# Cross-attention on one core: one load queue in order of use, 40 idle transposes, and the last context rows turned between A and U

## The chip, the cores and the metric

The kernel runs on one core of one Trainium2 chip. The metric is device time in microseconds (us) of that core for one execution. Three runs of the kernel before gave 289.30, 289.48 and 289.98 us, a median of 289.48 us.

## What is computed

A cross-attention layer with a residual and a layer norm, in float32, over 16 batches, with 256 queries and 77 context rows for each and 8 heads of width 256. The mask of the inputs is all ones.

```python
Q = (x @ Wq).reshape(B, -1, H, D)            # x: (16, 256, 256), Wq: (256, 2048)
K = (ctx @ Wk).reshape(B, -1, H, D)          # ctx: (16, 77, 192), Wk: (192, 2048)
V = (ctx @ Wv).reshape(B, -1, H, D)          # Wv: (192, 2048)
score = einsum('bhqd,bhkd->bhqk', Q, K) / sqrt(256)    # heads moved ahead of the rows
attn = softmax(where(mask, score, -inf))
out = einsum('bhqk,bhkd->bqhd', attn, V).reshape(B, -1, H * D) @ Wo + x
y = (out - mean(out)) * rsqrt(var(out) + 1e-5) * gamma + beta
```

## The kernel before

The products of the weights are formed first, so that the big activations meet small matrices only. For each head, G = Wk Wq^T / 16 (192 x 256) stands for the query and key projections, and U = Wv Wo (192 x 256) for the value and output projections. Then, for four batches at a time, "A" is the context times G (77 columns for each head and batch); the scores of a batch are x times A, and the output is the probabilities times (context times U).

The work is in two stages. The first, the prologue, loads all weights, forms G and U, turns the context so that its columns lie on the partitions, and prepares A for the first four batches. The second, the loop over batches at L639, does scores, softmax, attention and layer norm; the prologue ends at about 61 us of 288.

The order of all engines is written by hand (`manual_schedule`, L80): each engine runs its instructions in the order of the program, and a tile framework adds the semaphore waits. Loads go through DMA instructions issued by the SP queue (SyncE) or, for one weight block, by the ACT queue. The framework counts their landings on eight semaphores taken in turn, so the ninth DMA can't be issued until the first has landed: at most eight loads are in flight.

The prologue, with the lines that matter here:

- `ident` is built on POOL; 28 transposes of `ident` into a bank that nobody reads follow on PE (L477-478).
- The weights Wk and Wq come in four column blocks a = 0..3 of four pieces each (`wk_nat`, 96 KB a piece, and `wq_nat`, 128 KB a piece; `load_qk`, L442-445). Block 0 of Wk is issued by ACT at the same time as block 0 of Wq by SP; all else is on SP.
- The context `c_sb` comes in two parts: its first three row blocks of 112 rows (252 KB, `load_c(0, first)`, L456) serve the first four batches; the other eight (672 KB, L459) the rest. Then come Wv (`wvT`, 16 pieces of 96 KB, L467), Wo (`wo_all`, 4 of 512 KB, L469), the mask (`bias`, 616 KB as broadcast), and x for the first group (`xT`).
- `wo_all` lies in the same memory as `wq_nat` (tag "w128"), so its first load waits until DVE has turned the last block of Wq.
- `turn_qk(a)` (L488) transposes block a of both weights in 32 x 32 blocks on DVE. `turn_v` (L514) does so with Wv.
- `turn_c(lo, hi)` (L495) turns row blocks of the context: transposes on PE into `pc` (L501), a copy to `cA` on ACT, one to the upper half of `cB` on DVE, and a copy of that to the lower half on POOL (L512).
- The loop over j = 0, 1 (L565) forms G for two of the four blocks (`pg`, L524, and `ph`, L538), scales it out of PSUM (`gA` on ACT, `gB` on DVE), and prepares half of A of the first four batches (`pa`, L184 and L198, then copies that alternate between ACT and DVE). For j = 0 the first context rows are turned between the two halves of `pg`, and at the end the remaining rows are turned (L593), followed on POOL by `cRA`, `cRB` (the last 13 keys of each batch) and a memset of `vr`.
- U follows (`pu`, L524, and `pw`, L538), and copies of `uB` on ACT, DVE and POOL (L619). POOL also makes `bias` from the mask (L602), ahead of the `uB` copies.
- `prepare_last` (L251) multiplies `cRA`/`cRB` with U into `pr` and copies it into `vr`.

PSUM is one ring of eight banks (`ps_mm`), taken in order.

```python
        load_qk(0, (nc.scalar, nc.sync))
        load_qk(1, (nc.sync, nc.sync))
        load_c(0, first)
        load_qk(2, (nc.sync, nc.sync))
        load_qk(3, (nc.sync, nc.sync))
        load_c(first, NCR)
```

Of the kernel before, what the change touches and what calls it, by code (L numbers as in the profile page):

```python
# [20 lines left out]
KM = 64  # L21
# [23 lines left out]
def kernel(  # L45
# [13 lines left out]
    nc = tc.nc  # L59
# [4 lines left out]
    NCR = B * S2 // CR  # L64
# [4 lines left out]
    NF = H // 2  # L69
    KR = S2 - KM  # L70
    BK = 32
    NM = P // BK
# [30 lines left out]
    cA = const.tile([P, B, S2], F32, tag="cA", name="cA")  # L103
    cB = const.tile([P, B, S2], F32, tag="cB", name="cB")
    cRA = const.tile([P, B, KR], F32, tag="cRA", name="cRA")
    cRB = const.tile([P, B, KR], F32, tag="cRB", name="cRB")
    vr = const.tile([P, B, DI], F32, tag="vr", name="vr")
# [13 lines left out]
    def flat(ap):  # L121
        return ap.rearrange("p a b -> p (a b)")
# [4 lines left out]
    def load_x(g):  # L127
        xg_of[g] = const.tile([P, GT, DI], F32, tag=f"xg{g}", name=f"xg_{g}")
        nc.sync.dma_start(xg_of[g], x_rows[:, g * GT : (g + 1) * GT, :])
# [3 lines left out]
    def evacuate(dst, src):  # L133
        evacs[0] += 1
        if evacs[0] % 2:
            nc.scalar.copy(dst, src)
        else:
            nc.vector.tensor_copy(dst, src)
# [295 lines left out]
    with tc.tile_pool(name="wonce", bufs=1) as wp:  # L434
        c_sb = wp.tile([CR, NCR, DL], F32, tag="c", name="c_sb")

        wq_nat = wp.tile([P, NF, DI // BK, P], F32, tag="w128", name="wq_nat")
        wk_nat = wp.tile([P, NF, NL, P], F32, tag="w96", name="wk_nat")
        wq_blocks = wq.rearrange("(m r) (a i f) -> a i r m f", r=BK, a=NF, i=NM)
        wk_blocks = wk.rearrange("(m r) (a i f) -> a i r m f", r=BK, a=NF, i=NM)  # L440

        def load_qk(a, queues):  # L442
            for queue, nat, blocks in zip(queues, (wk_nat, wq_nat), (wk_blocks, wq_blocks)):
                for i in range(NM):
                    queue.dma_start(nat[i * BK : (i + 1) * BK, a], blocks[a, i])

        def load_c(lo, hi):
            nc.sync.dma_start(c_sb[:, lo:hi, :], c_rows[:, lo:hi, :])

        first = -(-GB * S2 // CR)  # L450
        load_qk(0, (nc.scalar, nc.sync))

        warm = wp.tile([P, 1], F32, tag="warm", name="warm")
        nc.scalar.activation(warm, eps, AF.Exp)
        load_qk(1, (nc.sync, nc.sync))
        load_c(0, first)  # L456
        load_qk(2, (nc.sync, nc.sync))
        load_qk(3, (nc.sync, nc.sync))
        load_c(first, NCR)  # L459

        wvT = wp.tile([P, NF, NL, P], F32, tag="wvT", name="wvT")
        wo_all = wp.tile([P, NF, 4, DI], F32, tag="w128", name="wo_all")
        wv_blocks = wv.rearrange("(m r) (a i f) -> a i r m f", r=BK, a=NF, i=NM)
        wo_rows = wo.rearrange("(a p n) f -> a p n f", p=P, n=4)
        for a in range(NF):
            for i in range(NM):
                nc.sync.dma_start(wvT[i * BK : (i + 1) * BK, a], wv_blocks[a, i])  # L467
        for a in range(NF):
            nc.sync.dma_start(wo_all[:, a], wo_rows[a])  # L469
        nc.sync.dma_start(  # L470
            bias_f.bitcast(I32), mask.rearrange("b k -> (b k)").partition_broadcast(P)
        )
# [1 line left out]


        idle = ps_mm.tile([P, P], F32, tag="mm", name="idle")
        for i in range(28):  # L477
            nc.tensor.transpose(idle, ident, ident)


# [7 lines left out]
        def turn_qk(a):  # L488
            for nat, of in ((wk_nat, wkT_of), (wq_nat, wqT_of)):
                nc.vector.transpose(  # L490
                    of[a // 2][:, a % 2].rearrange("p n (m r) -> p m n r", r=BK),
                    nat[:, a].rearrange("p m (n c) -> p m n c", c=BK),
                )

        def turn_c(lo, hi):  # L495
            for r in range(lo, hi, 2):
                n = min(2, hi - r)
                pc = ps_mm.tile([P, 4, P], F32, tag="mm", name=f"pc_{r}")
                for lc in range(2):
                    for j in range(n):  # L500
                        nc.tensor.transpose(  # L501
                            pc[:, 2 * lc + j, :CR],
                            c_sb[:, r + j, lc * LB : lc * LB + P],
                            ident[:CR, :CR],
                        )
                rows = slice(r * CR, (r + n) * CR)
                evacuate(flat(cA)[:, rows].rearrange("p (j m) -> p j m", m=CR), pc[:, :n, :CR])
                evacuate(
                    flat(cB)[LB:, rows].rearrange("p (j m) -> p j m", m=CR),
                    pc[LB:, 2 : 2 + n, :CR],  # L510
                )
                nc.gpsimd.tensor_copy(flat(cB)[:LB, rows], flat(cB)[LB:, rows])  # L512

        def turn_v(a):  # L514
            blocks = wvT[:, a].rearrange("p m (c n) -> p m n c", n=4)
            nc.vector.transpose(blocks, blocks)
# [3 lines left out]
        def of_pair(out, a, weight, moving):  # L520

            for n in range(4):
                for e in range(2):
                    nc.tensor.matmul(  # L524
                        out[e][:, a % 2, :],
                        weight(a, e, n)[:, :P],
                        moving(a, e, n),
                        start=(n == 0),
                        stop=(n == 3),
                    )  # L530

        def rest_of_pairs(j, weight, moving, name):

            banks = [ps_mm.tile([P, DI], F32, tag="mm", name=f"{name}_{j}_{e}") for e in range(2)]
            for n in range(4):
                for i in range(2):
                    for e in range(2):
                        nc.tensor.matmul(  # L538
                            banks[e][half(i)],
                            weight(2 * j + i, e, n)[:, P:],  # L540
                            moving(2 * j + i, e, n),
                            start=(n == 0),
                            stop=(n == 3),
                        )
            return banks

        def two_banks(name, j):
            return [ps_mm.tile([P, 2, DI], F32, tag="mm", name=f"{name}_{j}_{e}") for e in range(2)]
# [16 lines left out]
        for j in range(NF // 2):  # L565
            pg = two_banks("pg", j)
            of_pair(pg, 2 * j, wk_part, wq_part)
            if j == 0:
                turn_c(0, first)
            of_pair(pg, 2 * j + 1, wk_part, wq_part)  # L570
            for e in range(2):
                nc.scalar.mul(gA_of[:, j, e], pg[e], D ** -0.5)
            for e, ph in enumerate(rest_of_pairs(j, wk_part, wq_part, "ph")):
                nc.vector.tensor_scalar(gB[:, 2 * j + e, :], ph, D ** -0.5, None, ALU.mult)
            if j == 0:
                turn_qk(2)
            else:
                turn_v(0)
                turn_v(1)
                for g in range(NG):  # L580
                    load_x(g)
                    if g == 0:
                        nc.sync.dma_start(gam, gamma.partition_broadcast(P))
                        nc.sync.dma_start(bet, beta.partition_broadcast(P))
            part_A, part_B, copies = prepare_a(0, (2 * j, 2 * j + 1))
            part_A()
            part_B()
            for i, (dst, src) in enumerate(copies()):
                evacuate(dst, src)
                if j == 0 and i == 3:  # L590
                    turn_qk(3)
            if j == 0:
                turn_c(first, NCR)  # L593
                nc.gpsimd.tensor_copy(cRA, cA[:, :, KM:])
                nc.gpsimd.tensor_copy(cRB, cB[:, :, KM:])
                nc.gpsimd.memset(vr, 0.0)
        turn_v(2)
        turn_v(3)

# [13 lines left out]
        for j in range(NF // 2):  # L613
            for e, pw in enumerate(rest_of_pairs(j, wv_part, wo_part, "pw")):
                for i, engine in enumerate((nc.scalar.copy, nc.vector.tensor_copy)):
                    a = 2 * j + i
# [118 lines left out]
```

## Time and profile before

| | |
|---|---|
| median of three runs | 289.48 us |
| the profiled execution: its time | 289.93 us |
| its span, first to last instruction | 288.1 us |
| PE busy | 275.2 us (96%) |
| DVE, ACT, POOL busy | 216.9, 113.1, 119.1 us |
| mean granted TensorE clock | 0.985 |
| loads and stores | 22.51 MB |

A line of a timeline gives the start and the length in us, the engine, the line of the kernel, the operation, what it writes and reads, the shapes and the number of instructions; the bracket at its end gives the idle time before it and what ended that. A line of the chain of waits gives start, length and what the end of the execution depended on in that stretch. A line of a table of windows gives, for a stretch of the span, each engine's busy time (and number of instructions), the granted TensorE clock (1.00 is full), the mean busy share of the 16 DMA engines and the rate of all transfers in GB/s. PE is matrix multiplication, PEld the loading of its weights, SPq and ACTq the queues that issue DMAs.

### The profile page before, as it was taken

To read this page: it belongs to the slowest core of one execution; us is meant where nothing else is said; L and a number is where in the kernel's file an instruction comes from. 1 tells how busy PE (TensorE), PEld (TensorE's weight loads), DVE (VectorE), ACT (ScalarE), POOL (GpSimd) and SP (SyncE) were. 2 spreads that over 40 slices of the span, in tenths; PEclk is the share of its full clock that TensorE was granted. 3 is DMA by queue.
4 is the path that set the end of the run, shared out by engine and by line. 5 is a ranking of instruction groups with operands and counts; after the bars stand their busy time and mean duration, and the time that the engine had idled before them with its cause. 6 is when DMAs were issued, how large, how long until landed. Compare 5 with 4: busy or idle time off the path is not lost.

```text
span 288.1 us, 11561 instructions
## 1 busy us (share of the span) xinstructions
PE 275.2 (96%) x5234; PEld 180.5 (63%) x5234; DVE 216.9 (75%) x421; ACT 113.1 (39%) x195; POOL 119.1 (41%) x150
## 2 busy tenths in 40 slices
PE   7598999999999999999999999999999999999990
PEld 7365669994757575757575757574757567575550
DVE  0536383755858798989797989897979898898884
ACT  2023221122353535353535353535353535635541
POOL 1000706705443434243434252534342528658474
PEclk9689999999999999999999999999999999999998
DMA  8999799994000101910000009000000010010112
GB/s 145 207 201 207 221 327 220 294 261 82 2 2 3 39 5 35 152 34 9 29 15 26 15 20 165 20 25 14 28 11 33 8 35 11 30 41 3 40 39 73
DMA packets 38498, 22.51 MB, mean 78 GB/s; under 512 B 17888, under 2 KB 37808, under 8 KB 38448
## 3 DMA queue, kind: packets, MB, share of 16 engines
q1 hardware_dynamic: 37616, 21.37, 33.9%
q8 instruction: 41, 0.67, 1.0%
q10 hardware_dynamic: 832, 0.39, 0.8%
q14 instruction: 9, 0.07, 0.1%
HBM read 17.57 MB, written 4.19 MB: 76 GB/s over the span
## 4 chain that ended last, share of the span: by engine, by line
PE 85%; DMA 8%; DVE 2%; POOL 2%; issue 1%; ACTq 0%; ACT 0%; SPq 0%; POOLq 0%
PE ps L297 23%; PE po L362 22%; PE pa L184 10%; PE pv L225 10%; PE pv L236 6%; DMA wk_nat<-in_L_xattn_Wk_dram 5%; PE pa L198 5%; DMA c_sb<-in_ctx_dram 3%; PE pu L524 3%; PE pr L258 2%; PE pw L538 1%; PE pg L524 1%; PE pr L268 1%; PE ph L538 1%; PE pc L501 1%; POOL xg L413 1%
## 5 line engine op out<-in xcount | busy, mean ns | idle before, releaser
L319 POOL TENSOR_TENSOR s<-s,top 128x616 f32<-128x616 f32 x32 | 38.9, 1216 | 90.8 <-DVE top L318 86.4
L297 PE MATMUL ps<-a,xT 128*32 128x154 f32 x2048 | 70.0, 294 | 0.0
L297 PEld LDWEIGHTS ps<-a,xT 128*32 128x32 f32 x2048 | 66.4, 110 | 3.5 <-issue 0.8
L340 POOL TENSOR_TENSOR p<-e,rden 128x512 f32<-128x512 f32 x64 | 50.1, 802 | 31.8 <-ACT a L673 27.0
L362 PE MATMUL po<-vw,pT 128*32 128x256 f32 x1024 | 61.5, 380 | 0.0
L362 PEld LDWEIGHTS po<-vw,pT 128*32 128x32 f32 x1024 | 31.8, 110 | 28.2 <-issue 5.5
L332 DVE TENSOR_REDUCE den<-e 128x8 f32<-128x616 f32 x32 | 25.3, 790 | 23.7 <-ACT e L326 23.7
L184 PE MATMUL pa<-cA,gA 128*32 128x308 f32 x512 | 35.8, 423 | 0.0
L326 ACT ACTIVATE e<-s 128x616 f32<-128x616 f32 x32 | 23.0, 719 | 28.7 <-POOL s L319 28.7
L671 ACT COPY vw<-pv 128x512 f32<-128x512 f32 x32 | 18.6, 581 | 36.2 <-PE pv L236 36.2
L311 DVE TENSOR_TENSOR s<-ps,bias 128x308 f32<-128x308 f32 x64 | 27.8, 465 | 4.2 <-PE ps L297 4.2
L225 PE MATMUL pv<-uA,cA 128*32 128x512 f32 x256 | 30.4, 592 | 0.0
L184 PEld LDWEIGHTS pa<-cA,gA 128*32 128x32 f32 x512 | 16.4, 110 | 20.9 <-issue 6.5
L419 DVE SCALAR_TENSOR_TENSOR xg<-xg,rstd,bet 128x256 f32<-128x256 f32 x25 | 27.9, 1116 | 0.9
L350 DVE STREAM_TRANSPOSE pT<-p 128x640 f32<-128x640 f32 x32 | 25.0, 810 | 2.5 <-POOL p L340 2.5
L387 ACT ACTIVATE std<-mv,eps 128x2 f32<-128x2 f32 (+1 forms) x17 | 5.0, 296 | 55.0 <-DVE mv L379 54.3
L318 DVE TENSOR_REDUCE top<-s 128x8 f32<-128x616 f32 x32 | 25.4, 795 | 1.1
L362 PE MATMUL po<-vr,pT 128*32 128x256 f32 x256 | 19.7, 379 | 0.0
L198 PE MATMUL pa<-cB,gB 64*32 64x308 f32 x512 | 19.5, 420 | 0.0
L387 ACT ACT_TABLE_LOAD x15 | 19.2, 1283 | 0.3
L326 ACT ACT_TABLE_LOAD x14 | 18.0, 1283 | 0.3
L236 PE MATMUL pv<-uB,cB 64*32 64x512 f32 x256 | 17.4, 601 | 0.0
(68 smaller groups left out, 271.9 us busy)
## 6 DMA issues: line engine op xcount, KB each, us to landing
xT<-in_x_dram SPq DMA_DIRECT2D x16, 256.0 KB, 7.0
xg<-in_x_dram SPq DMA_DIRECT2D x4, 1024.0 KB, 9.2
out_dram<-xg SPq DMA_DIRECT2D x15, 256.0 KB, 2.2
wq_nat<-in_L_xattn_Wq_dram SPq DMA_DIRECT2D x16, 128.0 KB, 4.5
wo_all<-in_L_xattn_Wo_dram SPq DMA_DIRECT2D x4, 512.0 KB, 5.4
wvT<-in_L_xattn_Wv_dram SPq DMA_DIRECT2D x16, 96.0 KB, 3.9
wk_nat<-in_L_xattn_Wk_dram SPq DMA_DIRECT2D x12, 96.0 KB, 4.5
c_sb<-in_ctx_dram SPq DMA_DIRECT2D x1, 672.0 KB, 8.4
```

The lines of the kernel that those rows point to most:

```text
L184: nc.tensor.matmul(flat(o[i * BK : (i + 1) * BK]), gA[:, h, cols(dc, i)], flat(cA[:, batches, :]), start=not B_first, stop=B_first,)
L198: nc.tensor.matmul(flat(banks[j + k][i * BK : (i + 1) * BK]), gB[half(k), h // 4 * 2 + h % 2, cols(dc, i)], flat(cB[half(k), batches, :]), ...
L225: nc.tensor.matmul(pv[k][i * BK : (i + 1) * BK], cA[:, b, k * BK : (k + 1) * BK], uA[:, :, :, i], start=True, stop=False,)
L236: nc.tensor.matmul(pv[k][i * BK : (i + 1) * BK], cB[half(k), b, k * BK : (k + 1) * BK], uB[half(k), :, :, i], start=False, stop=True,)
L297: nc.tensor.matmul(ps[m // 2][i * BK : (i + 1) * BK, m % 2 * 2 * S2 : (m % 2 + 1) * 2 * S2], xT_of[g][:, j * NM + m, dc], flat(a_of[g][:, ...
L311: nc.vector.tensor_tensor(s[:, a * H // 2 : (a + 1) * H // 2], ps[a][:, : H // 2 * S2].rearrange("p (h k) -> p h k", k=S2), bias[:, b, :]. ...
L318: nc.vector.tensor_reduce(top, s, AX.X, ALU.max)
L319: nc.gpsimd.tensor_tensor(s, s, top.unsqueeze(2).to_broadcast([P, H, S2]), ALU.subtract)
L326: nc.scalar.activation(e, s_of.pop(t), AF.Exp)
L340: nc.gpsimd.tensor_tensor(part, e_mh[:, :, :, keys], rden_mh.unsqueeze(3).to_broadcast(list(part.shape)), ALU.mult,)
L362: nc.tensor.matmul(po[i * BK : (i + 1) * BK], pT[:, n, i], vw_of[b][:, n // 2, n % 2, :] if n < NF else vr[:, b, :], start=(n == 0), stop= ...
L419: nc.vector.scalar_tensor_tensor(y, y, rstd, bet, ALU.mult, ALU.add)
```

## The change

Three things are changed, all in the prologue.

1. All loads ahead of the loop are issued by SP. The order is now Wk block 0, Wq block 0, Wk block 1, the first context rows, Wq block 1, blocks 2 and 3, Wv, Wo, and only then the other context rows, followed by the mask and x as before. The function `load_blocks` loads one block of any of the three weights in four pieces. Sizes and the number of transfers stay the same.
2. There are 40 idle transposes in place of 28.
3. The remaining context rows are turned after the loop over j (after the second half of A) and ahead of U, together with `cRA`, `cRB` and the memset of `vr`, in place of the end of the pass j = 0.

```diff
-        def load_qk(a, queues):
-            for queue, nat, blocks in zip(queues, (wk_nat, wq_nat), (wk_blocks, wq_blocks)):
-                for i in range(NM):
-                    queue.dma_start(nat[i * BK : (i + 1) * BK, a], blocks[a, i])
+        def load_blocks(nat, blocks, a):
+            for i in range(NM):
+                nc.sync.dma_start(nat[i * BK : (i + 1) * BK, a], blocks[a, i])
...
-        load_qk(0, (nc.scalar, nc.sync))
+        load_blocks(wk_nat, wk_blocks, 0)
+        load_blocks(wq_nat, wq_blocks, 0)
+        load_blocks(wk_nat, wk_blocks, 1)
+        load_c(0, first)
+        load_blocks(wq_nat, wq_blocks, 1)
+        for a in range(2, NF):
+            load_blocks(wk_nat, wk_blocks, a)
+            load_blocks(wq_nat, wq_blocks, a)
...
-        load_qk(1, (nc.sync, nc.sync))
-        load_c(0, first)
-        load_qk(2, (nc.sync, nc.sync))
-        load_qk(3, (nc.sync, nc.sync))
-        load_c(first, NCR)
...
         for a in range(NF):
-            for i in range(NM):
-                nc.sync.dma_start(wvT[i * BK : (i + 1) * BK, a], wv_blocks[a, i])
+            load_blocks(wvT, wv_blocks, a)
         for a in range(NF):
             nc.sync.dma_start(wo_all[:, a], wo_rows[a])
+        load_c(first, NCR)
...
-        for i in range(28):
+        for i in range(40):
             nc.tensor.transpose(idle, ident, ident)
...
-            if j == 0:
-                turn_c(first, NCR)
-                nc.gpsimd.tensor_copy(cRA, cA[:, :, KM:])
-                nc.gpsimd.tensor_copy(cRB, cB[:, :, KM:])
-                nc.gpsimd.memset(vr, 0.0)
+        turn_c(first, NCR)
+        nc.gpsimd.tensor_copy(cRA, cA[:, :, KM:])
+        nc.gpsimd.tensor_copy(cRB, cB[:, :, KM:])
+        nc.gpsimd.memset(vr, 0.0)
```

## The prediction

> **What bounds the kernel now.** I read the page first: PE is busy 96% of the span and the chain of waits is PE from 27.1 us to 272 us without a gap. So a change to the prologue counts for exactly what it moves the start of U (`pu`): everything from there to the end follows as one block. Then I read the chain up to U.
>
> ```profile
> 14.01 4.56 DMA wk_nat<-in_L_xattn_Wk_dram
> 18.59 8.42 DMA c_sb<-in_ctx_dram
> 27.14 1.72 PE pc L501 x16
> 28.86 3.65 PE pg L524 x32
> 32.52 1.89 PE ph L538 x32
> 34.41 4.28 PE pa L184 x64
> 38.69 2.23 PE pa L198 x64
> 40.92 7.77 PE pu L524 x64
> ```
>
> To be seen: until 27.0 us the end hangs on loads, the last being the 672 KB of context; then PE runs through to U at 40.92. PE's timeline shows what it did before that:
>
> ```profile
> 1.34 5.61 PE L478 MATMUL idle<-ident 128*128 128x128 f32 x28 [1.34 <-POOL ident masks.py:199]
> 10.45 3.79 PE L524 MATMUL pg<-wqT,wkT 64*128 64x256 f32 x16 [3.50 <-DVE wqT L490]
> 14.16 1.38 PE L501 MATMUL pc<-ident,c_sb 112*128 112x112 f32 x6
> 15.47 2.43 PE L524 MATMUL pg<-wqT,wkT 64*128 64x256 f32 x16
> ```
>
> The first 16 `pg` took 3.79 us, while 32 of the same took 3.65 us later. The windows say why, and give the load rates:
>
> ```profile
> 2.00:8.00 6.00, 4.95 (x27) 4.71 (x25) 0.00 (x0) 1.49 (x2) 0.00 (x0) 1.00 1.18 200
> 9.00:10.00 1.00, 0.00 (x0) 0.00 (x0) 1.00 (x2) 0.00 (x0) 0.00 (x0) 0.79 1.23 201
> 10.00:16.00 6.00, 5.55 (x24) 4.09 (x26) 2.91 (x5) 0.60 (x2) 0.00 (x0) 0.50 1.21 206
> 17.00:22.00 5.00, 5.00 (x78) 2.78 (x78) 2.15 (x4) 1.08 (x2) 0.00 (x0) 1.00 1.22 202
> 22.00:24.00 2.00, 2.00 (x34) 0.78 (x24) 0.61 (x1) 0.00 (x0) 0.00 (x0) 1.00 1.10 251
> 27.00:30.00 3.00, 2.86 (x28) 2.64 (x30) 2.97 (x7) 1.39 (x4) 0.86 (x3) 1.00 0.64 161
> 34.00:40.00 6.00, 6.00 (x120) 2.84 (x120) 4.36 (x5) 0.44 (x2) 0.64 (x1) 1.00 1.02 392
> ```
>
> The clock is at half from 9.6 to 16.4 us, after 3.5 us without PE work. Weights in small pieces come at 0.20 MB/us, context at 0.25, Wo at about 0.40. From 27 to 34 us the DMA engines are half idle: a hole. Last, the waits and the DVE and POOL rows I need:
>
> ```profile
> SPq L467 <- DMA c_sb<-in_ctx_dram: 2.9, 1, 2.9
> ...
> 26.70 1.20 DVE L490 STREAM_TRANSPOSE wqT<-wq_nat 128x1024 f32<-128x1024 f32 x1
> ...
> 31.14 3.50 POOL L596 MEMSET vr<- 128x4096 f32 x1
> 43.21 4.38 POOL L602 TENSOR_SCALAR bias<-bias 128x1232 f32<-128x1232 int32 x1 [8.57 <-DMA bias<-in_mask_BxS_if_dram]
> 51.19 3.57 POOL L619 COPY uB<-uB 64x256 f32<-64x256 f32 x8 [3.60 <-ACT uB L618]
> ```
>
> **What the Trainium skill says.** "TensorE: Matmul & The Clock Gate", Part 1: the clock is halved after an idle window of some 3.4 us and restored after a busy one. The trace agrees: halved at 9.6 us, two such windows at half (6.8 us). Its Part 4 says transposes don't count as activity; this trace disagrees, for the clock record rises at 6.2 us with nothing but the 28 transposes run so far. "DMA: Bandwidth & Descriptors", section "Issuing engines are not separate DMA queues": loads from two queues share the same 16 DMA engines and a second queue saves only issue time. The trace agrees: 200 GB/s with two queues filled (2 to 8 us), 202 with one. The same page ("Why a DMA increments its semaphore by 16 and not by 1") says a transfer has landed only when each of its engines has reported, so the slowest decides. The semaphore record agrees: 15 of 16 reports of the 672 KB context are in by 25.3 us and the last comes at 27.0.
>
> **Part 1, the loads.** Nothing is removed but the use of ACT's queue: its four issues (1.90 us at 0.71) now precede Wq's on SP. An issue takes about 0.49 us, so SP fills 96 KB in 0.49 us, just the 0.20 MB/us that the engines take: cost about nothing, at most the 1.9 us of issue if the engines ran dry, at least a small gain because Wk and Wq no longer interleave. Sums from the sizes, with the first packet at 2.0 us and 0.9 us from last packet to report (as c's first part shows: packets to 12.5, report at 13.46): Wk 0 and Wq 0 (0.92 MB) by 7.5, and I keep the 8.1 us of before; first context rows (1.57 MB) 10.7; Wq 1 (2.09 MB) 2.0 + 10.5 + 0.9 = 13.4 us, against 12.4 before; block 3 (3.93 MB) data by 21.6, as before.
>
> From there the order differs. Wv 1.57 MB / 0.20 = 7.9 us, to 29.5; Wo 2.10 / 0.40 = 5.2, to 34.7; the 672 KB (0.69 MB) / 0.25 = 2.8, to 37.5; plus 0.9: landed at 38.4 us. SP's 2.9 us wait for the context in the middle of Wv, and the hole behind it, go; Wo thereby comes 4 us sooner. Wo's first issue still waits for `turn_qk(3)`; that ends at 27.9 before, 26.5 after (below), and the eight-in-flight limit lets Wo go at about 27.5 anyway, with 2 us of Wv still queued, so nothing is lost there. Behind Wo stand the context, mask and x; each has slack: x is turned at 54.97 without a wait.
>
> **The straggler.** The DMA record has a 16 KB instruction packet at 20.8, 28.8 and 39.3 us, and after each one engine reports late: Wq's last piece has 15 reports at 22.6 and the last at 23.8; for the context behind it the lag is 1.7 us; over the pieces of Wv it shrinks. PE is then at a fixed place in its program: the third falls in the second half of A, in the changed kernel about 35.5 us, just when the context moves. Bounds for the landing: 38.0 us (no lag, a little faster start) and 40.1 (38.4 + 1.7). The packet need not hit the same engine that is last; I take 38.6.
>
> **Part 2, the transposes.** Twelve more: 25 run at 0.20 us until the clock rises at about 6.2, the rest at about 0.12 (an estimate from `pc`: 16 in 1.72 us for 112 columns), ending near 8.4 us. The first `pg` can begin at 8.1 + 1.2 (one Wq transpose, 1.20 us) = 9.3, so they delay nothing, and PE is idle 0.9 us in place of 3.5. I take the clock to stay full: `pg` 1.83 (half of 3.65) to 11.1, `pc` 0.65 to 11.8, then a wait of 2.9 us for Wq 1, turned at 13.4 + 1.25 = 14.65. That wait is under 3.5 us; if it still halves the clock, the cost is up to 2 us here.
>
> **PE to the end of A.** Second `pg` 14.7 to 16.5, `ph` 1.89 to 18.4, A 4.28 + 2.23 to 24.9 (26.3 before: 1.4 us sooner). DVE's `turn_qk(3)` moves with A's copies, to 26.5; the second `pg` pair needs it at 26.75. Without the 16 `pc` (1.72) and their wait (0.83) between: `pg` 3.65, `ph` 1.89, A 6.51: A ends at 37.0, not 40.92. PSUM banks are free: the copies that free those of `pc` come from the first half of A's banks.
>
> **Part 3, the turn.** `pc` now waits for the context: on PE, U and all behind it stand queued. Start 38.7, 16 transposes 1.72, U at 40.4. That is 0.5 us ahead of 40.92: of the 3.9 us that PE gains, 1.7 go into the moved turn and 1.7 into a new wait. On DVE, `turn_v(2)` now follows four `cB` copies (1.32) and is done 2.8 us into U; U needs it at 3.9. On POOL, from the end of `pc`: copies, `cRA`, `cRB` and memset take 5.78 us (28.86 to 34.64), mask 4.38: done at +10.2. The `uB` copies start 10.27 us after U's start (51.19 - 40.92): just covered, with 0.6 us more before `pr` needs them (54.76 against 55.38). Here I take nothing; the cover is thin, and beyond 0.7 us POOL's delay would be PE's. The mask lands at about 42, far ahead of its use.
>
> **Sum.** U 0.5 us sooner: the profiled execution would take 289.4, not 289.93; it lies 0.45 above the median, so the median goes from 289.48 to 289.0.
>
> **Rivals.** (a) The likeliest, above: the load of the context takes the place of the waits removed; 289.0, its own range 288.4 to 289.6. Chance 0.45. (b) The loads keep up (no lag, faster start, context in by 37.5 or so): PE decides, U at 37.0 to 37.8 + 1.75, a gain of 1.4 to 2.2; about 287.7. For it: the hole in 27 to 34 is gone, DMA engines at 0.64 there. Against: the sum of bytes gives 38.4. Chance 0.25. (c) Slower: the straggling engine. The context lands at 40.1, U at 40.2 + 1.72 = 41.9, 1.0 us late: 290.5. It decides from a landing after 39.1 (40.92 - 1.72 - 0.1). For it: the third packet's time, no hole in which the engine catches up. Against: the lag shrank while Wv was moving. Chance 0.25. (d) The 40 transposes don't keep the clock, or POOL is late: hidden in (a) up to 1.6 us by the wait for the context, beyond it slower by some tenths; 0.05.
>
> **Chances.** A measurement of this kernel tells 0.2% (0.58 us) from no change. Faster: half of (a) and (b), 0.47. Same: the other half of (a), some of (c) and (d), 0.30. Slower: 0.23. The range takes in (b) and (c): 287.6 to 290.6.
>
> **What would show it.** Right: full clock from 6 us on; `pg` 1.8 us; A's end near 37; an idle of 1 to 2 us before 16 `pc` that a context DMA ends; U near 40.4; no SP wait inside Wv. (b) shows as no idle before `pc`; (c) as a landing after 39.1. I am wrong if PE waits between U and the loop, or if the loop itself changes length.

## The result, and the profile after

The changed kernel is slower: 292.29 us median (290.46 to 295.76, 20 runs) against 289.70 us of the kernel before in the same sessions; ratio 1.0076, 95% interval 1.0049 to 1.0104. The forecast was 289.0 us, with a range up to 290.6. The profiled execution has a span of 292.2 us, 4.1 more than before; such an execution is one draw from a wide scatter, so the ratio gives the size and the profile the places. Ratios leave out single runs that lie more than 1.5% above the fastest of their kernel (294.94 and 295.76 here).

The chain of waits of the changed kernel, from the end of the loads to `pr` (start, length, what the end hung on):

```profile
27.72 1.13 DVE wqT L491
30.77 10.96 DMA c_sb<-in_ctx_dram
41.86 1.78 PE pc L502 x16
43.64 9.10 PE pu L525 x57
52.73 3.68 PE pw L539 x64
56.41 3.01 PE pr L258 x16
```

U starts at 43.64 us (before: 40.92), and takes 9.10 us (7.77). That is 2.72 and 1.33 us, together 4.05; from `pw` on every length is that of before, and the loop starts 4.04 us late (65.45 against 61.41). So all that this execution loses is in two places: the start of `pc`, and the speed of `pu`. PE's timeline shows what came ahead:

```profile
1.34 6.76 PE L479 MATMUL idle<-ident 128*128 128x128 f32 x40 [1.34 <-POOL ident masks.py:199]
9.10 2.00 PE L525 MATMUL pg<-wqT,wkT 64*128 64x256 f32 x16 [1.00 <-DVE wqT L491]
11.66 0.79 PE L502 MATMUL pc<-ident,c_sb 112*128 112x112 f32 x6 [0.56 <-DMA c_sb<-in_ctx_dram]
15.22 2.98 PE L525 MATMUL pg<-wqT,wkT 64*128 64x256 f32 x16 [2.77 <-DVE wqT L491]
18.13 2.61 PE L539 MATMUL ph<-wqT,wkT 64*64 64x256 f32 x32
...
37.01 2.30 PE L198 MATMUL pa<-cB,gB 64*32 64x308 f32 x64
41.86 1.78 PE L502 MATMUL pc<-ident,c_sb 112*128 112x112 f32 x16 [2.54 <-DMA c_sb<-in_ctx_dram]
43.57 9.17 PE L525 MATMUL pu<-wo_all,wvT 64*128 64x256 f32 x64
```

The first `pg` took 2.00 us, not 3.79. But after the wait of 2.77 us the second `pg` took 2.98 and `ph` 2.61 (2.00 and 1.96 at full clock), and after the wait of 2.54 us `pu` was slow. A ended at 39.32 us, 1.6 us sooner than before, and then PE waited for the context. The windows (the last three columns are clock, share of the DMA engines, GB/s):

```profile
10.00:16.00 6.00, 2.67 (x26) 1.93 (x24) 2.81 (x4) 0.50 (x2) 0.26 (x1) 1.00 1.22 208
16.00:17.00 1.00, 1.00 (x8) 0.84 (x6) 0.00 (x0) 0.00 (x0) 0.34 (x2) 0.54 1.22 206
...
27.00:30.00 3.00, 3.00 (x34) 2.48 (x28) 2.59 (x4) 0.67 (x2) 0.00 (x0) 1.00 0.45 102
30.00:34.00 4.00, 4.00 (x62) 2.27 (x62) 1.15 (x3) 1.09 (x2) 0.00 (x0) 1.00 0.95 331
34.00:40.00 6.00, 5.32 (x112) 2.41 (x104) 4.68 (x6) 1.68 (x4) 0.00 (x0) 1.00 1.07 306
40.00:42.00 2.00, 0.14 (x2) 0.17 (x3) 0.00 (x0) 0.00 (x0) 0.00 (x0) 1.00 1.20 223
42.00:46.00 4.00, 4.00 (x28) 3.37 (x29) 3.07 (x6) 1.39 (x4) 2.54 (x7) 0.67 0.98 124
46.00:50.00 4.00, 4.00 (x34) 3.82 (x32) 2.26 (x3) 0.59 (x1) 3.91 (x2) 0.90 1.15 183
```

The clock record of the trace gives the edges: halved from 16.09 to 19.50 us and from 43.39 to 46.81. Each halving comes a little after PE has begun to work again (at 15.22 and 41.86 us), so the work behind a wait pays for it. From 27 to 30 us there is still a hole in the loads (102 GB/s).

### The profile page after: what moved, and what is told of

Its sections match the earlier page's. It is cut to its first block, busy times and chain, and to the rows that moved or that the text cites. A ratio compares the mean times of both kernels' runs of the same rounds, so it can differ in the third digit from the quotient of the medians.

```text
span 292.2 us, 11583 instructions
## 1 busy us (share of the span) xinstructions
PE 276.7 (95%) x5246; PEld 181.1 (62%) x5246; DVE 217.6 (74%) x421; ACT 113.1 (39%) x195; POOL 119.5 (41%) x150
## 4 chain that ended last, share of the span: by engine, by line
PE 80%; DMA 8%; SPq 5%; DVE 2%; POOL 2%; issue 1%; ACT 0%; POOLq 0%
PE ps L297 23%; PE po L362 21%; PE pv L225 9%; PE pa L184 9%; PE pv L236 6%; PE pa L198 4%; SPq L444 4%; DMA c_sb<-in_ctx_dram 4%; DMA wq_nat<-in_L_xattn_Wq_dram 3%; PE pu L525 3%; PE pr L258 2%; PE pw L539 1%; PE pr L268 1%; DMA wvT<-in_L_xattn_Wv_dram 1%; PE pc L502 1%
## 5 line engine op out<-in xcount | busy, mean ns | idle before, releaser
L318 DVE TENSOR_REDUCE top<-s 128x8 f32<-128x616 f32 x32 | 25.5, 795 | 1.1
L513 POOL COPY cB<-cB 64x224 f32<-64x224 f32 (+1 forms) x6 | 2.1, 357 | 41.4 <-DVE cB L138 41.3
```

Source lines behind the costliest of these rows:

```text
L318: nc.vector.tensor_reduce(top, s, AX.X, ALU.max)
```

## The experiments

Every kernel is compared with the kernel before on the same chip. Reports are the semaphore increments by which the 16 DMA engines tell that their part of a transfer has landed; "8th" is the middle one. U's start and the reports are those of one profiled execution each. For e2 that was the slowest of its four runs (295.55 us), and e3, e9 and e11 have four runs each too. Times in us.

| run | median | ratio to before, 95% interval | U starts (profile) | context: 8th and 16th report |
|---|---|---|---|---|
| changed kernel | 292.29 | 1.0076 (1.0049 to 1.0104) | 43.6 | 39.3, 41.7 |
| e1 context ahead of Wv | 289.73 | 1.0002 (0.9983 to 1.0021) | 40.4 | 24.5, 26.0 |
| e2 half of Wo not held | 291.96 | 1.0102 (1.0036 to 1.0169) | 45.3 | 39.1, 43.2 |
| e3 both waits filled | 295.29 | 1.0186 (1.0130 to 1.0243) | 45.9 | 39.9, 42.6 |
| e4 one queue and 40 transposes | 289.79 | 0.9997 (0.9972 to 1.0023) | 40.7 | 24.8, 25.5 |
| e5 no wait for the context | 290.36 | 0.9997 (0.9974 to 1.0019) | 40.9 | 39.5, 41.5 |
| e6 context between Wv and Wo | 289.84 | 0.9982 (0.9960 to 1.0005) | 38.8 | 34.5, 36.3 |
| e7 before with 40 transposes | 289.70 | 0.9987 (0.9967 to 1.0008) | 40.3 | 24.9, 26.4 |
| e8 e1, first wait filled | 288.35 | 0.9935 (0.9916 to 0.9954) | 39.8 | 25.2, 26.2 |
| e9 first wait filled | 295.37 | 1.0186 (1.0136 to 1.0235) | 45.8 | 39.7, 42.5 |
| e10 28 transposes | 293.18 | 1.0108 (1.0082 to 1.0134) | 43.5 | 39.1, 40.9 |
| e11 instruction packets shifted | 295.31 | 1.0195 (1.0147 to 1.0243) | 45.4 | 39.8, 42.4 |
| e12 e8, Wq 1 ahead of context | 287.92 | 0.9929 (0.9903 to 0.9954) | 38.6 | 25.4, 26.5 |

**e1: the context ahead of Wv, all else as changed.**

```diff
         for a in range(2, NF):
             load_blocks(wk_nat, wk_blocks, a)
             load_blocks(wq_nat, wq_blocks, a)
+        load_c(first, NCR)
...
             nc.sync.dma_start(wo_all[:, a], wo_rows[a])
-        load_c(first, NCR)
```

> The changed kernel, but with the 672 KB of context loaded ahead of Wv again; one queue, 40 idle transposes and the turn ahead of U stay. Theory (the late landing of the context at 41.7 us costs the 2.5 us wait of PE and, through it, the half clock in pu): the context lands by 27 us, pc follows A without a wait, pu takes 7.8 and not 9.1 us; U at about 41, 3.5 to 4 us less than the changed kernel's profile, so about the time of before (289.0 to 289.8). Rival (turning the rows right ahead of U costs by itself, on DVE or POOL): no wait before pc, but PE waits inside pu or before pr, time at 291 or more.

The loss is gone, and with it the wait. PE's timeline of e1:

```profile
14.63 3.68 PE L525 MATMUL pg<-wqT,wkT 64*128 64x256 f32 x16 [2.90 <-DVE wqT L491]
...
36.48 2.30 PE L198 MATMUL pa<-cB,gB 64*32 64x308 f32 x64
38.71 1.75 PE L502 MATMUL pc<-ident,c_sb 112*128 112x112 f32 x16
40.40 7.84 PE L525 MATMUL pu<-wo_all,wvT 64*128 64x256 f32 x64
```

`pc` follows A at once and `pu` takes 7.84 us. The turn right ahead of U costs nothing by itself that shows. One line of the change, the place of one transfer in the queue, makes the difference between the changed kernel and the time of before.

**e5: the same loads in the changed order, and nobody waits for the last.** The turn ahead of U reads the first three row blocks again, so this kernel leaves out the context of the later batches.

```diff
-                            c_sb[:, r + j, lc * LB : lc * LB + P],
+                            c_sb[:, (r + j) % 3, lc * LB : lc * LB + P],
```

> The changed kernel with all its loads in its order, but the turn ahead of U reads the first three row blocks in place of the eight that are loaded last (rows beyond the first four batches are thus replaced; the late rows are still loaded, and no engine waits for them there). Theory (the whole loss is PE's wait for the last engine of that load, and the half clock after it): PE runs from A into pc, U at 41.0, pu 7.8 us, a gain of 3.5 to 4 us in the profile and about 2 to 2.5 us in the median: the time of before within 0.5 us. Rival (the later Wo or the turn in this place costs as well): over 1 us above before.

PE's timeline of e5:

```profile
39.18 1.75 PE L502 MATMUL pc<-ident,c_sb 112*128 112x112 f32 x16
40.86 7.84 PE L525 MATMUL pu<-wo_all,wvT 64*128 64x256 f32 x64
```

The context came as late as in the changed kernel (last report at 41.5), and the time is that of before. So nothing else in the new order costs anything that the interval (0.9974 to 1.0019) would show; the wait, with what it does to the clock, is the loss.

**e4: one queue and 40 transposes, context and turn where they were.** It is e1 with the turn and its POOL work put back at the end of the pass j = 0.

> The changed kernel with the remaining rows loaded ahead of Wv and turned at the end of the pass j = 0, as before: what is left of the change is the one queue with its order and the 40 transposes. Theory (these two are worth little, the loss is that of the context moved behind Wo): the landing of the context at about 27 us decides as before, time within 0.6 us of before. Rival (one queue or the new order costs by itself, for instance through the wait of PE for Wq block 1, behind which the clock is halved): 1 us or more above before.

The same as before, within the interval. The rival, a cost of 1 us or more, falls.

**e7: before with 40 transposes.** The edit is `range(28)` to `range(40)`.

> The kernel before with 40 idle transposes and nothing else. Theory (in before the landing of the context at 27 us holds PE, so a full clock ahead of it is hidden): the clock stays full or drops only after the first pg, pg takes 2.0 us and not 3.8, A's first half ends 1 us sooner or more, pc waits for the context that much longer; same time as before within 0.3 us. Rival (the transposes are worth what they save in pg): 0.5 to 1 us less than before.

The same time within the interval, as expected. PE's timeline of e7 shows the hidden gain:

```profile
10.28 2.00 PE L524 MATMUL pg<-wqT,wkT 64*128 64x256 f32 x16 [1.89 <-DVE wqT L490]
13.56 0.80 PE L501 MATMUL pc<-ident,c_sb 112*128 112x112 f32 x6 [1.28 <-DMA c_sb<-in_ctx_dram]
14.29 2.00 PE L524 MATMUL pg<-wqT,wkT 64*128 64x256 f32 x16
...
26.53 1.72 PE L501 MATMUL pc<-ident,c_sb 112*128 112x112 f32 x16 [1.84 <-DMA c_sb<-in_ctx_dram]
```

The first half of A ended at 24.7 us in place of 26.3, and the wait for the context grew from 0.83 to 1.84 us. That wait did not halve the clock: the 32 `pg` behind it took 3.72 us (3.73 in before). U came 0.6 us sooner (40.25 against 40.85) because the context happened to land at 26.4 us, not 27.0.

**e10: the changed kernel with 28 transposes.** The edit is `range(40)` to `range(28)`.

> The changed kernel with 28 idle transposes. Theory (the transposes act only on work that the context's landing covers): pg at 9 us runs at half clock or not, A ends at 39 to 40 us, landing as late as in the changed kernel; time within 0.6 us of it. Rival (the 12 transposes, by their 24 PE instructions or by the clock, are a part of the loss): 1 us or more less.

No gain: the rival falls, and the interval overlaps that of the changed kernel, though the median is 0.9 us higher and not within the 0.6 us expected. PE's timeline of e10:

```profile
9.09 2.00 PE L525 MATMUL pg<-wqT,wkT 64*128 64x256 f32 x16 [3.11 <-DVE wqT L491]
14.78 3.48 PE L525 MATMUL pg<-wqT,wkT 64*128 64x256 f32 x16 [2.97 <-DVE wqT L491]
41.01 2.57 PE L502 MATMUL pc<-ident,c_sb 112*128 112x112 f32 x16 [2.29 <-DMA c_sb<-in_ctx_dram]
```

PE was idle for 3.11 us ahead of the first `pg`, and the clock still stayed up until 14.4 us. So in the changed kernel, too, it isn't shown that the 12 transposes are what made the first `pg` fast.

**e2: half of Wo in memory of its own.**

```diff
-        wo_all = wp.tile([P, NF, 4, DI], F32, tag="w128", name="wo_all")
+        wo_two = [
+            wp.tile([P, 2, 4, DI], F32, tag="wo01", name="wo_01"),
+            wp.tile([P, 2, 4, DI], F32, tag="w128", name="wo_23"),
+        ]
```

> The changed kernel with the first half of Wo in memory of its own, so that its first two loads no longer wait for turn_qk(3) on DVE. Theory (Wo is held until 28.9 us by memory shared with wq_nat, the DMA engines run dry from 27 to 30 us, and the context behind Wo is late by that): the load rate from 27 to 30 us rises from 102 to over 200 GB/s, the context lands 1 to 2 us sooner, 0.8 to 2.8 us less than the changed kernel, the upper end if the wait before pc gets too short to halve the clock. Rival (the context is late by the slow engine that reports last, whatever stands before it): landing within 0.5 us of 41.7, no gain.

My theory fell. The rate from 27 to 30 us rose to 169 GB/s only, the middle report came at 39.1 (39.3 in the changed kernel), and the last at 43.2, where the 15th stood at 39.95: a single engine was 3.3 us behind all others. The rival had no gain right, but not its landing within 0.5 us of 41.7. That Wo is held by `turn_qk(3)` in the changed kernel is true (it ends at 28.84, Wo is issued at 28.93), and freeing half of it moved the middle report by 0.2 us only.

**e3 and e9: PE kept busy in its waits.** e9 fills the first wait, e3 both.

```diff
+        def fill(n):
+            spare = ps_mm.tile([P, P], F32, tag="mm", name="spare")
+            for i in range(n):
+                nc.tensor.transpose(spare, ident, ident)
...
             if j == 0:
                 turn_c(0, first)
+                fill(20)
```

> The changed kernel with 20 more transposes of ident in each of the two waits of PE (before the second half of pg, and before pc of the remaining rows). Theory (the two waits of 2.8 and 2.5 us halve the clock): granted clock 1.00 throughout after 6 us; pg and ph after the first wait take 1.9 us each and not 3.0 and 2.6, turn_qk(3) ends 1.5 to 1.9 us sooner and with it Wo and the context; pu takes 7.8 and not 9.1 us: 2.5 to 3.5 us less than the changed kernel. Rival (the clock costs nothing, PE just waits for loads): pu shorter, but its start as late as in the changed kernel or later by what the transposes take; gain under 1 us.

> The changed kernel plus 20 transposes of ident in the first wait of PE only (before the second half of pg). Theory (the landing of the context decides when pc starts, whatever PE has done by then): A ends at about 37.9 us in place of 39.25, the context still lands at 41.5 us or later, the wait before pc grows by what A gains, and the time is not less than the changed kernel's. Rival (the half clock after the first wait is part of the loss): 1 us or more less than the changed kernel.

In e3 I had expected a gain and got a loss. The first filling did hold the clock, and A ended sooner (38.0 and 37.4 us, against 39.32). But the context landed at 42.6 and 42.5, so PE waited for the load, as the rival of e3 and the theory of e9 have it; neither forecast the size of the loss, 3 us against the changed kernel. The second filling of e3 did not hold the clock. PE's timeline of e3:

```profile
37.92 2.40 PE L484 MATMUL spare<-ident 128*128 128x128 f32 x20
42.73 3.22 PE L507 MATMUL pc<-ident,c_sb 112*128 112x112 f32 x16 [2.41 <-DMA c_sb<-in_ctx_dram]
```

The 20 transposes ended 2.4 us ahead of `pc`, and the clock fell at 42.43 us. PE's timeline of e9, and its windows:

```profile
14.99 2.00 PE L530 MATMUL pg<-wqT,wkT 64*128 64x256 f32 x16 [0.51 <-DVE wqT L496]
...
35.15 2.30 PE L198 MATMUL pa<-cB,gB 64*32 64x308 f32 x64
42.60 3.22 PE L507 MATMUL pc<-ident,c_sb 112*128 112x112 f32 x16 [5.15 <-DMA c_sb<-in_ctx_dram]
45.75 8.49 PE L530 MATMUL pu<-wo_all,wvT 64*128 64x256 f32 x64
```

```profile
37.40:42.60 5.20, 0.05 (x9) 0.03 (x1) 0.63 (x2) 0.46 (x2) 0.00 (x0) 0.81 1.15 245
42.60:46.00 3.40, 3.40 (x18) 3.12 (x20) 1.18 (x3) 1.18 (x4) 0.80 (x3) 0.50 0.78 115
46.00:50.00 4.00, 4.00 (x30) 3.74 (x32) 3.53 (x3) 0.20 (x1) 3.56 (x5) 0.81 0.99 181
```

What A gains turns into wait, and a wait of 5.15 us costs more than one of 2.54: `pc` runs at half clock too (3.22 us in place of 1.78). Against the changed kernel's profile U starts 2.2 us later, 1.4 of it from `pc` and 0.7 from the landing. Why the landing was later is not shown.

**e6: the context between Wv and Wo.**

```diff
             load_blocks(wvT, wv_blocks, a)
+        load_c(first, NCR)
...
             nc.sync.dma_start(wo_all[:, a], wo_rows[a])
-        load_c(first, NCR)
```

> The changed kernel with the context rows between Wv and Wo. Theory (the amount of data ahead of the rows and the engine that lags decide, 2.1 MB of Wo are 6 us): the rows land at 33 to 36 us, ahead of A's end at 39; Wo is late by 3 us but its first block lands by 37 and its last by 43, each before pu needs it; the time of before within 0.5 us. Rival (only the place in the queue right ahead of the mask or the use right after landing matters, or pu now waits for Wo): pu starts late or stretches, 1 us or more above before.

The time of before, as expected. PE's timeline of e6:

```profile
14.76 2.00 PE L525 MATMUL pg<-wqT,wkT 64*128 64x256 f32 x16 [2.65 <-DVE wqT L491]
37.15 1.75 PE L502 MATMUL pc<-ident,c_sb 112*128 112x112 f32 x16
38.83 7.84 PE L525 MATMUL pu<-wo_all,wvT 64*128 64x256 f32 x64
```

The context landed at 36.3 us and PE came to it at 37.15. That is under 1 us of slack, and it was enough in this execution.

**e11: the instruction packets shifted.**

```diff
-        for i in range(40):
+        for i in range(20):
             nc.tensor.transpose(idle, ident, ident)
+        for i in range(80):
+            nc.tensor.transpose(idle[:BK, :BK], ident[:BK, :BK], ident[:BK, :BK])
```

> The changed kernel with 20 of the idle transposes as they are and the other 20 replaced by 80 of 32 x 32, which take about as long: 60 more transposes, 120 more PE instructions, so the 16 KB instruction packets (17.7, 26.9, 38.4 us in the changed kernel) come some 3 us sooner and the third falls into Wo or the context. Theory (each such packet holds up one DMA engine by about 1.2 us, and the last engine decides): the context's last report comes 0.5 to 2 us later than 41.7 us or the one engine lags more, time 0.5 to 2 us more than the changed kernel. Rival (the lag has other grounds, the engines drift apart by themselves in a queue that never runs dry): landing at 41.2 to 42.2, same time as the changed kernel.

The third packet came at 34.2 us. The second block of Wo had all 16 reports by 34.3; the third had 15 by 35.6 and the last at 37.3. The context had 15 by 40.4 and the last at 42.4. The landing moved by 0.7 us, in the expected direction. The profiled executions differ by 0.7 us as well (294.70 against 293.97), but the medians by 3.0, which the landing doesn't explain. Nor did the edit move the packets alone, as PE's timeline of e11 shows:

```profile
5.59 2.50 PE L481 MATMUL idle<-ident 32*32 32x32 f32 x80
9.13 3.47 PE L527 MATMUL pg<-wqT,wkT 64*128 64x256 f32 x16 [1.03 <-DVE wqT L493]
```

The clock was halved from 8.73 to 12.15 us, though the small transposes had kept PE at work until 8.1 us.

In e9 the packet came at 35.1 and in e3 at 35.7, and the last engine fell behind in Wo's third (e9) or fourth block (e3); where it came at 38.4 to 39.0 (changed kernel, e5, e10) the landing was at 40.9 to 41.7. That speaks for the packets as one ground of the lag, and isn't proof. In the changed kernel the last report of Wo's fourth block already came 1.8 us behind the 15th (38.71 against 36.93), and that block's last packet had gone out at 37.22 us, ahead of the instruction packet at 38.37. e2, with the packet at 39.6, had the largest lag of all, and in e5 the middle and the 14th report lie 1.2 us apart. Why the last engine lags stays open.

**e8 and e12: a version that beats both.** e8 is e1 with `fill(20)` as in e9. e12 also puts the first context rows behind Wq block 1 in the queue, turns them behind the second half of `pg`, and has 16 transposes in the wait. The edits of e12, without the place of the context rows, which is that of e1:

```diff
+        load_blocks(wq_nat, wq_blocks, 1)
         load_c(0, first)
-        load_blocks(wq_nat, wq_blocks, 1)
...
             if j == 0:
-                turn_c(0, first)
+                fill(16)
             of_pair(pg, 2 * j + 1, wk_part, wq_part)
+            if j == 0:
+                turn_c(0, first)
```

> Run e1 (one queue, context ahead of Wv, turn ahead of U, 40 transposes) plus 20 transposes of ident in the wait before the second half of pg. Theory (with the context early no load holds PE between the second half of pg and U, so here a full clock pays): the clock does not drop at 14.8 us, the second half of pg takes 1.9 to 2.0 us and not 3.7, U starts 1.0 to 1.7 us sooner than in e1, at about 39; Wo's first block (35 us in e1) is in time: 288.0 to 288.8. Rival (Wo or turn_v holds pu): U as early but pu longer, the gain under 0.4 us.

> Run e8 with the first context rows loaded after Wq block 1 and turned after the second half of pg, 16 transposes in the wait. Theory (in e8 PE still waits for Wq block 1 until 15.7 us, behind 252 KB of context): Wq block 1 is turned about 1 us sooner, pg's second half starts at 14.4 to 14.8, U about 0.7 us sooner than in e8: 287.4 to 288.2. Rival (then Wo's blocks or the turning of Wv decide): the same as e8 within 0.3 us.

Both times came as the theory had it: 0.9935 and 0.9929 of before. That e12 beats e8 is not shown, since the intervals overlap almost wholly. U in e8 was 0.6 us sooner than in e1, less than the 1.0 to 1.7 expected, since Wq block 1 came later in that execution (second half of `pg` at 15.73 us, 14.63 in e1); in the profile of e12 it was 1.2 us sooner than in e8. The filling that lost time in e9 gains it in e8; the only difference is where the context stands in the queue. PE's timeline of e12:

```profile
11.13 1.97 PE L484 MATMUL spare<-ident 128*128 128x128 f32 x16
13.83 2.00 PE L530 MATMUL pg<-wqT,wkT 64*128 64x256 f32 x16 [0.74 <-DVE wqT L496]
...
36.95 1.75 PE L507 MATMUL pc<-ident,c_sb 112*128 112x112 f32 x16
38.63 7.84 PE L530 MATMUL pu<-wo_all,wvT 64*128 64x256 f32 x64
```

No load holds PE between the second half of `pg` and U, so each tenth gained at 14 us is still there at U: in e6 and e8, both at full clock, U follows 24.1 us after it.

## Why the prediction was wrong

**The mechanism was named, its size was off.** "The load of the context takes the place of the waits removed" is what happened, and the rival (c) named the engine that reports last. The term that failed is the landing of the context: taken at 38.6 us, with bounds of 38.0 and 40.1; measured 41.7, and 40.9 to 43.2 in the seven profiles in which it stands behind Wo. That is 3.1 us over the 38.6. Two parts of the sum were too small.

- The middle of the engines, 0.9 us. The sum without a lag is "landed at 38.4"; the middle report came at 39.3. Wo's first packet went out at 29.93 us, not 29.5, and its last block's middle report came 6.5 us later, at 36.39, where the sum has 5.2 + 0.9 = 6.1 us. In the kernel before it was 33.15 to 39.54, 6.4 us. Behind Wo the context took 2.95 us, not 2.8. The rate of 0.40 MB/us was read from a window that begins at 34 us and leaves out the slow start of the transfer (139 GB/s from 33.5 to 34.0 us); the packets of before, looked at singly, would have told it.
- The last engine, 2.2 us. I gave it 0.2 us over the sum, though the profile of before showed 1.7 over the 15th report and 1.9 over the middle, on the ground that the lag shrank over Wv. Why it shrank there is not shown: it fell from 1.6 to 0.9 us over Wv's first seven pieces, and the queue ran dry at 27.5 us. In the changed kernel the engines are busy from 30 us up to the context, and the lag over the middle was 2.4 us, of which 0.9 stood between the 8th and the 14th report, so it was not one engine alone. The upper bound of 40.1 was the wrong one too: over the middle, the seven profiles showed 1.8 to 4.1 us.

**The clock: two steps fell, one with no number in the sum.** "That wait is under 3.5 us" (the wait ahead of the second `pg`, 2.77 us) did halve the clock. It cost 1.0 us in `pg` and 0.7 in `ph`, as the "up to 2 us here" said, and with Wq block 1 turned 0.5 us late it is why A ended at 39.3 and not at 37.0 us. It was hidden by the wait for the context, as rival (d) said and e9 shows. The second wait, ahead of `pc`, I had priced as a wait alone; that it halves the clock for `pu` is 1.33 us which no case held. "The Trainium skill", page "TensorE: Matmul & The Clock Gate", Part 1, states that the window of some 3.4 us runs freely and doesn't start with the work. The trace agrees: the edges at 5.85, 16.09, 19.50, 43.39 and 46.81 us lie on one grid of 3.413 us. What failed is the reading that a window has to be idle as a whole. The window from 12.67 to 16.09 held 2.55 us of the wait (12.45 to 15.22), and the clock fell; the second wait had 1.88 us in the window from 39.98, and it fell again. The profile of before had it already: in the window that ended with the halving at 9.57 us, PE worked for the first 0.8 us. So the length of a wait doesn't decide by itself. In e6 a wait of 2.65 us lay across an edge (13.13), at most 1.6 us in one window, and the clock stayed; so it did in e10 with 3.11 us (1.6 and 1.5). What share of a window is enough, these runs don't settle: 1.84 us in one window of e7 left the clock up, and in e11 it fell after a window with only 0.6 us of idle time, most of it filled with 32 x 32 transposes. The grid lies elsewhere in every execution: its first edge is at 4.2 us in one profile and at 7.1 in another. That fits the wide scatter of the single times, and is not shown to be all of it.

**What held.** The first `pg` (2.00 us; forecast 1.83) and its start (9.10; 9.3). `pc`'s length. Wq block 1, turned at 15.2 (14.65). POOL's cover: the `uB` copies still waited for ACT, 1.69 us. No wait between U and the loop, whose length is the same. Wrong, and of little consequence: `turn_qk(3)` at 28.84 (26.5 forecast), so that Wo was held after all; in e2, with half of it freed, Wo's first packet went out at 29.51 us and not 29.93, and nothing was gained. The 40 transposes were summed to 8.4 us, but the terms (25 at 0.20 and 15 at 0.12 us from 1.34 us on) give 8.1, as measured. The third instruction packet came at 38.4 us (35.5 forecast).

**From the profile to the ratio.** Forecast for U was 40.4; it started at 43.64 (3.2 us) and `pu` took 1.33 more: 4.5 us between forecast and this execution. The medians differ by less, 2.6 us against the 0.5 us of gain that was forecast, 3.1 in all; the profiled execution lies 1.7 us above the median (293.97 us). That the grid spares one of the waits in some executions would explain it, and was not tried.

## What to carry to other kernels

A transfer that an engine waits for has landed when the slowest of its DMA engines has reported; behind the long queue of these runs that was 1.8 to 4.1 us after the middle engine, so leave it that slack or put it ahead of loads which have some. Ask what holds the chain before an engine is made faster in front of it: filling PE's wait lost time with the context late (e9 against the changed kernel) and gained about 0.7% with the context early (e8, 0.9935 of before, against e1, 1.0002). A wait of PE can cost more than its length: here 1.9 us of one clock window of 3.4 were enough to halve the clock, and the work behind the wait pays.

## What the runs showed of the hardware

- The clock changes on a grid of 3.413 us. It fell after 1.88 us of idle time in one cell (the second wait of the changed kernel) and stayed after 1.6 us (e6) and 1.84 us (e7, the wait ahead of `pc`). The last two figures lie too close to the first to say that idle time alone decides.
- 128 x 128 transposes of `ident` keep the clock up: in e8 and e12 nothing else ran in the wait. The Trainium skill has the contrary ("TensorE: Matmul & The Clock Gate", Part 4, on the transpose mode). Small ones did not: in e11, 80 of 32 x 32 took 2.50 us, and the clock fell at 8.73 us.
- One DMA engine of 16 can be 3.3 us behind the next slowest in one transfer of 672 KB (e2), while the other 15 report within 1.3 us.
- A lag of one engine starts at a 16 KB instruction packet in several places (before at 20.8 us, e11 at 34.2), and without one in Wo's third and fourth block of the changed kernel.
